# A Strassen-Winograd graph network: M2 accumulated onto M1's copy in PSUM, M5 kept where C22 is built, and W1 read into the room of another tile

## The chip, the cores and the metric

The kernel runs on one core of one Trainium2 chip. The time is device time in microseconds: 2273.53 us, the median of three runs (2271.55 to 2274.96). The profile shows one execution with a span of 2271.4 us. The core has a matrix engine (TensorE, PE in the profile), a vector engine (DVE), a scalar engine (ACT), GpSimd (POOL) and SyncE (SP), which issues most transfers here. They run side by side, each through its own queue in order, and wait for each other on semaphores.

## The reference

Two layers of a graph network, 32 graphs of 512 nodes with 512 features, all in float32:

```
h = relu(layernorm(x));  deg = rowsum(adj)
x = x + relu(concat(h, (adj @ h) / max(deg, 1e-6)) @ W.T)
h = relu(layernorm(x));  q, k = split(h @ Wqk);  v = h @ Wv
w = mask * rowsum(q * (adj @ (k * mask))) / sqrt(512)
x = x + softmax(w over nodes) * v
```

## The kernel before

**Rearranged algebra.** W falls into W1 (for h) and W2 (for the aggregate). Layer 0 first computes `y` = h W2, then `out` = h W1 + A y, with A the adjacency divided by its degrees; relu and the residual follow. In layer 1, q · (adj k) is taken as a row sum of t and u, with `u` = A times the masked h1, and t = h1 (Wq Wk^T); v = h1 Wv. The product of Wq and Wk is made once, so t and v come from one product, `tv`, whose right side holds both matrices side by side (tile `mv`).

**Seven products in place of eight.** Each 512 x 512 product is cut into 2 x 2 blocks and done with seven block products M1 to M7 of Winograd's form of Strassen's algorithm; in `tv` the inner blocks are cut the same way again. Sums of blocks of the left and of the right side (`left_sums`, `right_sums`, L102 to L113, four DVE operations each) are stored in seven slots. The four result blocks share partial sums: M1 + M2 is C11; M1 + M6 is the start of the other three; M1 + M6 + M7 + M5 is C22; M1 + M6 + M5 + M3 is C12; M1 + M6 + M7 + M4 is C21.

**`product` (L118 to L162)** writes this as a generator: it yields after each group of matmuls, so that other work can be put between. It takes three PSUM tiles of one bank each. `pp` gathers M1, then M6, M7 and M4 on top; `pr` holds M2; `pq` holds M5 and then M3. Between these, ACT copies the state of `pp` to SBUF (C11, C12 and C22 so far) and M5 to a block of its own (`m5`), and DVE adds: C11 = copy + `pr`, C22 = copy + `m5`, C12 = copy + `pq`. C21 is taken from `pp` by ACT. The order is M1, M2, M6, M5, M7, M3, M4. In `y` and `u` a block product is 4 matmuls (8 records, as a float32 matmul shows as two); in `out` it is twice that, one half for each of its two terms. `into` (L420) gives where `y` and `u` put the blocks; `layer0_out` (L435) puts them in `block` tiles of the tag `tmp` (four buffers) and adds relu of them to X. `layer1_tv` (L451) is the same scheme with four banks for each of `pp`, `pr` and `pq`; there M5 also goes to blocks, and C22 is `pp` + M5. `layer1_one` does t and v apart, for the last two batches alone.

**Loop.** For batch i the phases follow each other: `out` of i; `tv` of i-1; `u` of i; `y` of i+1. `run` (L167) steps through a phase's generator, and after step n it issues what a `Plan` holds for n. So the order in every queue is written out by hand. A `finish` of a product is issued when its generator is resumed: after the plan's work of that step. In `u`, ahead of C22's add, the plan has DVE turn h1 (`f.turn`), undo the second Strassen level for the lower rows (`post.recombine`, 7 adds) and form four row sums (`post.dot`, L608). In `y` it has DVE turn the adjacency (`fb.turn`), add the softmax terms and undo the level for v.

**W1** does not fit beside everything else. Its seven slots are kept in device memory, and `Stream` (L400) reads them again for each batch into four buffers: four loads are issued at step 0 of `u`, three at steps 1, 3 and 5 of `out`. `tv` (L675) is one tile of 128 x 2 x 2 x 14 x 128 values: row halves, then t or v, then 14 columns of blocks. The t part is last read by `post.dot` in `u` and is written again in the next `tv`.

PSUM is one pool of eight banks (`ps_m`, L72).

Of the kernel before, what the change touches and what calls it, by code (L numbers as in the profile page):

```python
# [16 lines left out]
P = 128  # L17
# [5 lines left out]
def kernel(  # L23
# [32 lines left out]

    nc = tc.nc
    B, N, F = x.shape  # L60
    C = N // P
# [7 lines left out]
    big = ctx.enter_context(tc.tile_pool(name="big", bufs=1))  # L69
    small = ctx.enter_context(tc.tile_pool(name="small", bufs=2))  # L70
    dram = ctx.enter_context(tc.tile_pool(name="dram", bufs=2, space=bass.MemoryType.DRAM))
    ps_m = ctx.enter_context(tc.tile_pool(name="ps_m", bufs=8, space=bass.MemoryType.PSUM))  # L72


    LEFT = {1: 0, 2: 1, 3: 2, 4: 3, 5: 4, 6: 5, 7: 6}
# [3 lines left out]

    PLACE = {2: 0, 3: 1, 4: 2, 7: 3, 1: 4, 6: 5, 5: 6}  # L80
    AT = {p: j for j, p in PLACE.items()}
    ORDER = [1, 2, 6, 5, 7, 3, 4]

    def slots(tag, bufs, name, pool=None):
        return (pool or big).tile([P, 7, 2, H], F32, tag=tag, bufs=bufs, name=name)

    def block(name):
        return big.tile([P, 2, H], F32, tag="tmp", bufs=4, name=name)

    def mm_tile(name):  # L90
        return ps_m.tile([P, 2, H], F32, tag="m", name=name)

    def add(o, a, b, on=None):
        (on or nc.vector).tensor_tensor(o, a, b, op=ALU.add)  # L94
# [4 lines left out]
    def copy(o, i):  # L99
        nc.scalar.activation(o, i, AF.Copy)  # L100
# [14 lines left out]
    def of(t):  # L115
        return lambda i: t[:, i]

    def product(name, terms, place, finish):  # L118

        def m(k, p, first):
            n = 0
            for lt, rt in terms:
                right = rt(k)
                for rc in range(2):
                    for dk in range(2):
                        nc.tensor.matmul(  # L130
                            p[:, rc, :],
                            lt[:, LEFT[k], dk, ts(rc, P)],
                            right[:, dk, :],
                            start=first and n == 0,
                            stop=True,
                            skip_group_check=True,
                        )
                        n += 1
                yield

        pp = mm_tile(f"pp_{name}")
        yield from m(1, pp, True)
        c11 = place(0, 0)
        copy(c11, pp)
        pr = mm_tile(f"pr_{name}")
        yield from m(2, pr, True)
        finish(0, 0, c11, pr, c11)
        yield from m(6, pp, False)
        c12 = place(0, 1)
        copy(c12, pp)  # L150
        pq = mm_tile(f"pq_{name}")
        yield from m(5, pq, True)
        m5 = block(f"m5_{name}")
        copy(m5, pq)
        yield from m(7, pp, False)
        c22 = place(1, 1)
        copy(c22, pp)
        finish(1, 1, c22, m5, c22)
        yield from m(3, pq, False)
        finish(0, 1, c12, pq, c12)  # L160
        yield from m(4, pp, False)
        finish(1, 0, None, pp, None)  # L162

    def right(t):
        return lambda k: t[:, RIGHT[k]]
# [11 lines left out]
    class Later:  # L177


        def __init__(self, tiles, c):  # L180
            self.tiles, self.c = tiles, c
# [103 lines left out]
    class FrontH:  # L285
# [8 lines left out]
        def load(self, h, t=None):  # L294
            self.n[h] = half_tile(f"n_{self.b}_{h}") if t is None else t
            half_rows(self.n[h], x[self.b], h)
# [103 lines left out]
    class Stream:  # L400


        def __init__(self):
            self.d = dram.tile([7, P, 2, H], F32, tag="dw1", bufs=1, name="dw1")
            self.tiles = []
            self.n = 0

        def load(self):
            k = ORDER[self.n % 7]
            t = big.tile([P, 2, H], F32, tag="w1", bufs=4, name=f"w1_{self.n}")  # L410
            nc.sync.dma_start(out=t, in_=self.d[RIGHT[k]])
            self.tiles.append((k, t))
            self.n += 1

        def take(self, k):
            want, t = self.tiles.pop(0)
            assert want == k
            return t

    def into(t):  # L420


        def finish(r, c, o, p, s):
            if s is None:
                copy(t[:, 2 * r + c, :, :], p)
            else:
                add(o, p, s)

        return (lambda r, c: t[:, 2 * r + c, :, :]), finish

    def layer0_y(b):
        y = Y[b] = slots("yh", 1, f"y_{b}")
        return product(f"y_{b}", [(hT, right(w2R))], *into(y))

    def layer0_out(b, w1):  # L435
        def place(r, c):
# [14 lines left out]
    def layer1_tv(b):  # L451

        t = TV[b] = tv
        left = H1T[b]

        def m(k, banks, first):
            for half in ((2, 1), (3, 0)):
                for n in half:  # L460
                    if first:
                        banks[n] = mm_tile(f"ptv_{b}_{k}_{n}")
                    for i, p in enumerate(range(2 * n, min(2 * n + 2, 7))):
                        j = AT[p]
                        nc.tensor.matmul(  # L465
                            banks[n][:, :, ts(i, P)],
                            left[:, LEFT[k], LEFT_IN[j], :],
                            mvR[:, RIGHT[k], RIGHT[j], :, :],
                            start=first and i == 0,
                            stop=True,  # L470
                            skip_group_check=True,
                        )
                yield half

        def part(o, n):
            first = [0, 4, 8, 10][n] + (2 if n < 2 else 3) * (o % 2)
            return t[:, o // 2, :, first:first + min(2, 7 - 2 * n), :].rearrange("p w b f -> p w (b f)")

        def parts(k, banks, first, use):
            for half in m(k, banks, first):  # L480
                yield
                for n in half:
                    use(n, banks[n][:, :, 0:P * min(2, 7 - 2 * n)])

        def keep(o):
            return lambda n, p: copy(part(o, n), p)

        def plus(o):
            return lambda n, p: add(part(o, n), p, part(o, n))

        pp, pr, pq, m5 = {}, {}, {}, {}

        def keep5(n, p):
            m5[n] = block(f"m5_tv_{b}_{n}")[:, :, 0:P * min(2, 7 - 2 * n)]
            copy(m5[n], p)

        yield from parts(1, pp, True, keep(0))
        yield from parts(2, pr, True, plus(0))
        yield from parts(6, pp, False, keep(1))
        yield from parts(5, pq, True, keep5)  # L500
        yield from parts(7, pp, False, lambda n, p: add(part(3, n), p, m5[n]))
        yield from parts(3, pq, False, plus(1))
        yield from parts(4, pp, False, keep(2))

    def layer1_one(b, which, held=None):
# [40 lines left out]
        def plus(o):  # L546
            return lambda n, p: add(part(o, n), p, part(o, n))

        pp, pr, pq, m5 = {}, {}, {}, {}

        def keep5(n, p):
            m5[n] = like(n, block(f"m5_w_{which}_{b}_{n}").rearrange("p a f -> p (a f)"))
            copy(m5[n], p)

        yield from parts(1, pp, True, keep(0))
        yield from parts(2, pr, True, plus(0))
        yield from parts(6, pp, False, keep(1))
        yield from parts(5, pq, True, keep5)
        yield from parts(7, pp, False, lambda n, p: add(part(3, n), p, m5[n]))
        yield from parts(3, pq, False, plus(1))  # L560
        yield from parts(4, pp, False, keep(2))

# [16 lines left out]
    class Post:  # L579
# [71 lines left out]
        def finish(self, r, c):  # L651

            v = self.blocks[r, c]
            for a in range(2):
                o = self.o[:, 2 * r + a, ts(c, H)]
                nc.vector.scalar_tensor_tensor(
                    o, v[:, a, :], self.sm[:, 2 * r + a:2 * r + a + 1], o, op0=ALU.mult, op1=ALU.add
                )
# [88 lines left out]
    def start():  # L747
# [42 lines left out]
            for k in range(2):  # L790
                turn_right(s2[h], h, k, w2R)
        for c in range(C):
            v = block(f"h_{c}").rearrange("p a f -> p (a f)")
            nc.scalar.activation(
                in_order(v), natural(X[0][:, c, :]), AF.Relu, scale=t[1][:, c:c + 1], bias=t[2][:, c:c + 1]
            )
            turn_chunk(v, c, "h")
# [7 lines left out]
        rows = {}  # L805

        def scale_a(c):
            rows[c] = block(f"a_{c}").rearrange("p a f -> p (a f)")
            nc.scalar.activation(
                in_order(rows[c]), natural(fa.n[c // 2][:, c % 2, :]), AF.Copy, scale=fa.rdeg[:, c:c + 1]  # L810
            )
# [122 lines left out]
    with tc.manual_schedule(engines=engines):  # L934
        weights, mvR = start()
        post = None
        for i in range(B):
# [4 lines left out]
            if i > 0:  # L942

                p = Plan()
                for n in range(3):
                    p.at(2 * n + 1, stream.load)
                right_y = right_sums(of(Y[i]))
                p.at(0, right_y[0])
                p.at(0, right_y[2])
# [45 lines left out]
                p.at(12, f.stats, 0)  # L995
                p.at(12, f.stats, 1)
                p.at(13, variance, f.t, 0, 2)
                run(layer0_out(i, stream.take), 14, p)


                post = Post(i - 1, F1[i - 1])
# [55 lines left out]
            if more:  # L1057
                p.at(0, f.turn, 0)
                p.at(1, f.turn, 1)
                p.at(2, FA[i + 1].to.read, 0)  # L1060
                p.at(3, FA[i + 1].to.read, 1)
                for n in range(4):
                    p.at(0, stream.load)
            if i == 0:
                fh = FH[2]
                for c in range(C):
# [38 lines left out]
            if more:  # L1105
# [3 lines left out]
                p.at(3, fb.turn, 1)  # L1109
                p.at(4, fb.sums, 0)  # L1110
                p.at(4, fb.sums, 2)
                p.at(1, load_x, i + 1)
                if i + 2 < B:
                    p.at(5, FH[i + 2].to.read, 0)
# [92 lines left out]
```

## Time and profile before

| | before |
|---|---|
| time, median of 3 | 2273.53 us |
| TensorE busy | 2259.1 us, 99% |
| weight loads (beside the matmuls) | 1978.7 us, 87% |
| DVE busy | 1923.6 us, 85%, 3803 instructions |
| ACT busy | 1025.6 us, 45%, 1896 instructions |
| POOL busy | 174.8 us, 8% |
| DMA, mean | 204 GB/s |
| ACT copies of `m5` in `y`, `u`, `out` | 32 each, 596 to 597 ns |
| DVE adds of C11 in `y`, `u`, `out` | 32 each, 690, 682, 674 ns |
| DVE adds of C22 in `y`, `u`, `out` | 32 each, 684, 684, 685 ns |
| W1 loads | 217 of 256 KB, 4.3 us from issue to landing (median) |

Rows of the profile in order of time have a start, a duration, the engine, the line, the operation, output and inputs by tile name, and in brackets how long the engine had stood idle and which instruction let it go on. Matmul ends are modelled, and a row of several (x8) runs from the first start to the last end, so the start of the next row is the surer number. A DVE record of 0.68 us is followed by the next after about 0.60. The chain is the work that ended last, traced back from the end. A line such as L94 is a helper (`add`), so one goes by the tile names: `xu` is the tile that holds X and later the result of `u`.

### The profile page before, as it was taken

The numbers are of one execution on the slowest core, as the hardware profiler recorded it, in microseconds if no ns is written. First come the engines' busy times: TensorE is split into PE (matmuls) and PEld (weight loads), VectorE is DVE, ScalarE is ACT, GpSimd is POOL, SyncE is SP. The second block draws the span as 40 slices with busy tenths as digits, with TensorE's granted clock in tenths as the row PEclk, the third lists the DMA queues.
The fourth block names the chain that finished last, engine by engine and source line by source line (L and its number), as shares of the span: only waits on it lengthen the run. The fifth ranks groups of instructions, "written<-read, shape, count | busy, mean of one in ns | idle before, by whom it ended". The sixth has DMA issues, their size and how long they took to land.

```text
span 2271.4 us, 32927 instructions
## 1 busy us (share of the span) xinstructions
PE 2259.1 (99%) x10550; PEld 1978.7 (87%) x10550; DVE 1923.6 (85%) x3803; ACT 1025.6 (45%) x1896; POOL 174.8 (8%) x260
## 2 busy tenths in 40 slices
PE   9999999999999999999999999999999999999998
PEld 7788888888888888888888888888888888888897
DVE  7798888888888888888888888888888888888778
ACT  4454443445434554444454344544444543445323
POOL 0000010000100000100000000000000010000000
PEclk9999999999999999999999999999999999999999
DMA  9978787887878777777878888777888787878543
GB/s 222 233 214 246 204 212 193 205 230 206 210 199 202 213 220 207 208 191 207 227 210 205 199 201 218 218 207 202 196 210 225 209 209 193 205 219 217 154 123 96
DMA packets 409773, 463.68 MB, mean 204 GB/s; under 512 B 37729, under 2 KB 271713, under 8 KB 405377
## 3 DMA queue, kind: packets, MB, share of 16 engines
q1 hardware_dynamic: 400192, 428.56, 69.5%
q0 software_dynamic: 8928, 32.51, 8.7%
q8 instruction: 83, 1.36, 0.3%
q14 instruction: 90, 0.73, 0.1%
q10 hardware_dynamic: 480, 0.52, 0.1%
HBM read 293.93 MB, written 167.51 MB: 203 GB/s over the span
## 4 chain that ended last, share of the span: by engine, by line
PE 93%; DMA 3%; DVE 2%; SPq 1%; ACT 0%; issue 0%; DVEq 0%; POOLq 0%; ACTq 0%
PE ptv L465 28%; PE pp_o L130 18%; PE pp_u L130 9%; PE pq_o L130 9%; PE pp_y L130 9%; PE pq_u L130 5%; PE pr_o L130 5%; PE pq_y L130 5%; PE pr_u L130 2%; PE pr_y L130 2%; PE pw L517 1%; DMA a<-in_adj_dram 1%; SPq L212 0%; DVE tv L94 0%; DMA room<-in_L_gnn_Wqk_dram 0%; DVE mv L97 0%
## 5 line engine op out<-in xcount | busy, mean ns | idle before, releaser
L465 PE MATMUL ptv<-mv,h1T 128*128 128x256 f32 x2940 | 639.7, 379 | 0.1
L465 PEld LDWEIGHTS ptv<-mv,h1T 128*128 128x128 f32 x2940 | 558.5, 190 | 76.4 <-DVE xu L444 0.5
L94 DVE TENSOR_TENSOR tv<-tv 128x256 f32<-128x256 f32 (+1 forms) x658 | 326.4, 508 | 13.4 <-ACT tv L100 1.5
L100 ACT ACTIVATE tv<-ptv 128x512 f32<-128x512 f32 (+1 forms) x360 | 184.9, 541 | 262.9 <-PE ptv L465 262.0
L130 PE MATMUL pp_y<-wide 128*128 128x256 f32 x1024 | 242.1, 379 | 1.5 <-ACT y L100 1.2
L130 PE MATMUL pp_u<-h1m,aT 128*128 128x256 f32 x1024 | 242.0, 379 | 0.0
L130 PE MATMUL pp_o<-y,aT 128*128 128x256 f32 x1024 | 241.9, 379 | 0.0
L130 PE MATMUL pp_o<-w,wide 128*128 128x256 f32 x992 | 234.3, 379 | 0.0
L130 PEld LDWEIGHTS pp_y<-wide 128*128 128x128 f32 x1024 | 194.2, 190 | 28.5 <-ACT y L100 1.6
L130 PEld LDWEIGHTS pp_u<-h1m,aT 128*128 128x128 f32 x1024 | 194.4, 190 | 27.0 <-issue 0.7
L130 PEld LDWEIGHTS pp_o<-y,aT 128*128 128x128 f32 x1024 | 194.5, 190 | 26.4
L130 PEld LDWEIGHTS pp_o<-w,wide 128*128 128x128 f32 x992 | 188.5, 190 | 25.6
L100 ACT ACTIVATE o<-pp_o 128x512 f32<-128x512 f32 x96 | 57.2, 596 | 296.0 <-PE pp_o L130 296.0
L100 ACT ACTIVATE y<-pp_y 128x512 f32<-128x512 f32 x128 | 76.3, 596 | 234.5 <-PE pp_y L130 233.4
L94 DVE TENSOR_TENSOR tv<-ptv,tv 128x512 f32<-128x512 f32 x240 | 139.6, 613 | 43.7 <-PE ptv L465 38.4
L97 DVE TENSOR_TENSOR h1T<-h1T 128x512 f32<-128x512 f32 (+2 forms) x193 | 165.8, 873 | 1.2
L100 ACT ACTIVATE xu<-pp_u 128x512 f32<-128x512 f32 x128 | 76.4, 597 | 195.9 <-PE pp_u L130 195.9
L246 POOL TENSOR_TENSOR rstd<-rstd,mhalf 128x2 f32<-128x2 f32 (+1 forms) x96 | 78.7, 820 | 651.0 <-DVE rstd L245 651.0
L130 PE MATMUL pq_y<-wide 128*128 128x256 f32 x512 | 121.0, 379 | 0.0
L130 PE MATMUL pq_o<-y,aT 128*128 128x256 f32 x512 | 121.0, 379 | 0.0
L130 PE MATMUL pq_u<-h1m,aT 128*128 128x256 f32 x512 | 121.0, 379 | 0.0
L94 DVE TENSOR_TENSOR tv<-ptv,m_tv 128x512 f32<-128x512 f32 (+1 forms) x120 | 72.0, 622 | 55.6 <-PE ptv L465 55.1
(130 smaller groups left out, 3269.4 us busy)
## 6 DMA issues: line engine op xcount, KB each, us to landing
w<-dw SPq DMA_DIRECT2D x217, 256.0 KB, 4.3
xu<-in_x_dram SPq DMA_DIRECT2D x128, 256.0 KB, 5.3
a<-in_adj_dram SPq DMA_DIRECT2D x256, 128.0 KB, 3.0
dh1T<-h1m SPq DMA_DIRECT2D x128, 256.0 KB, 3.1
dx<-xu SPq DMA_DIRECT2D x32, 1024.0 KB, 5.1
sh1T<-dh1T SPq DMA_DIRECT2D x256, 128.0 KB, 3.3
shT<-dhT SPq DMA_DIRECT2D x248, 128.0 KB, 6.0
daT<-a SPq DMA_DIRECT2D x124, 256.0 KB, 3.0
```

The source lines that it names most:

```text
L94: (on or nc.vector).tensor_tensor(o, a, b, op=ALU.add)
L97: (on or nc.vector).tensor_tensor(o, a, b, op=ALU.subtract)
L100: nc.scalar.activation(o, i, AF.Copy)
L130: nc.tensor.matmul(p[:, rc, :], lt[:, LEFT[k], dk, ts(rc, P)], right[:, dk, :], start=first and n == 0, stop=True, skip_group_check=True,)
L246: nc.gpsimd.tensor_tensor(rstd[:, a:b], rstd[:, a:b], mhalf[:, a:b], op=ALU.pow)
L465: nc.tensor.matmul(banks[n][:, :, ts(i, P)], left[:, LEFT[k], LEFT_IN[j], :], mvR[:, RIGHT[k], RIGHT[j], :, :], start=first and i == 0, st ...
L517: nc.tensor.matmul(banks[n][:, ts(i, P)], held[:, s, :] if held is not None and j == 3 else left[:, s, LEFT_IN[j], :], mvR[:, RIGHT[k], RI ...
```

## The change

Three things are done together. M2 is accumulated onto a copy of M1 that ACT puts straight into a PSUM bank (`pr`), so that this bank holds C11 when M2 is done; that needs one bank of its own (`ps_r`), with seven left in the other pool. In the first `y` M2 starts its bank afresh as before. M5 comes second instead of fourth and is copied by ACT to the place of C22; after M7 DVE adds `pp` to it, so the separate block and one copy go. And W1's slots are read, all seven, during `y` into the t part of `tv`, which is idle then; the four buffers go. The two spare `tmp` blocks go too, and at the start the turned rows use `tv` as well. The aim is fewer operations on ACT and DVE, less SBUF, and loads of W1 that wait for no buffer.

```diff
-    ps_m = ctx.enter_context(tc.tile_pool(name="ps_m", bufs=8, space=bass.MemoryType.PSUM))
+    ps_m = ctx.enter_context(tc.tile_pool(name="ps_m", bufs=7, space=bass.MemoryType.PSUM))
+    ps_r = ctx.enter_context(tc.tile_pool(name="ps_r", bufs=1, space=bass.MemoryType.PSUM))
...
-    ORDER = [1, 2, 6, 5, 7, 3, 4]
+    ORDER = [1, 5, 6, 2, 7, 3, 4]
...
         pp = mm_tile(f"pp_{name}")
         yield from m(1, pp, True)
-        c11 = place(0, 0)
+        pr = seed_tile(f"pr_{name}")
+        c11 = pr if seed else place(0, 0)
         copy(c11, pp)
-        pr = mm_tile(f"pr_{name}")
-        yield from m(2, pr, True)
-        finish(0, 0, c11, pr, c11)
+        pq = mm_tile(f"pq_{name}")
+        yield from m(5, pq, True)
+        c22 = place(1, 1)
+        copy(c22, pq)
         yield from m(6, pp, False)
         c12 = place(0, 1)
         copy(c12, pp)
-        pq = mm_tile(f"pq_{name}")
-        yield from m(5, pq, True)
-        m5 = block(f"m5_{name}")
-        copy(m5, pq)
+        yield from m(2, pr, not seed)
+        if seed:
+            finish(0, 0, None, pr, None)
+        else:
+            finish(0, 0, c11, pr, c11)
         yield from m(7, pp, False)
-        c22 = place(1, 1)
-        copy(c22, pp)
-        finish(1, 1, c22, m5, c22)
+        finish(1, 1, c22, pp, c22)
         yield from m(3, pq, False)
         finish(0, 1, c12, pq, c12)
         yield from m(4, pp, False)
...
+        def slot(self, k):
+            n = 2 * ORDER.index(k)
+            return tv[:, :, 0, n:n + 2, :].rearrange("p r i f -> p r (i f)")
+
+        def load(self, n):
+            nc.sync.dma_start(out=self.slot(ORDER[n]), in_=self.d[RIGHT[ORDER[n]]])
...
-                        banks[n] = mm_tile(f"ptv_{b}_{k}_{n}")
+                        banks[n] = (seed_tile if n == 0 and k != 1 else mm_tile)(f"ptv_{b}_{k}_{n}")
...
-        yield from parts(5, pq, True, keep5)
-        yield from parts(7, pp, False, lambda n, p: add(part(3, n), p, m5[n]))
+        yield from parts(5, pq, True, keep(3))
+        yield from parts(7, pp, False, plus(3))
...
-                for n in range(3):
-                    p.at(2 * n + 1, stream.load)
...
-                for n in range(4):
-                    p.at(0, stream.load)
...
+                for n in range(7):
+                    p.at(n, stream.load, n)
```

More of the change, by code (lines that the diff above doesn't have):

```diff
@@ L87, in block, with seed_tile @@
     def block(name):
-        return big.tile([P, 2, H], F32, tag="tmp", bufs=4, name=name)
+        return big.tile([P, 2, H], F32, tag="tmp", bufs=2, name=name)
     def mm_tile(name):
         return ps_m.tile([P, 2, H], F32, tag="m", name=name)
+    def seed_tile(name):
+        return ps_r.tile([P, 2, H], F32, tag="r", name=name)
     def add(o, a, b, on=None):
@@ L116, in of, with product @@
         return lambda i: t[:, i]
-    def product(name, terms, place, finish):
+    def product(name, terms, place, finish, seed=True):
         def m(k, p, first):
@@ L404, in __init__ @@
             self.d = dram.tile([7, P, 2, H], F32, tag="dw1", bufs=1, name="dw1")
[L405 to L418, printed above, removed]
+        def slot(self, k):
[3 more added lines that the diff above has]
+            nc.sync.dma_start(out=self.slot(ORDER[n]), in_=self.d[RIGHT[ORDER[n]]])
     def into(t):
@@ L432, in layer0_y @@
         y = Y[b] = slots("yh", 1, f"y_{b}")
-        return product(f"y_{b}", [(hT, right(w2R))], *into(y))
+        return product(f"y_{b}", [(hT, right(w2R))], *into(y), seed=b > 0)
     def layer0_out(b, w1):
@@ L489, in plus @@
             return lambda n, p: add(part(o, n), p, part(o, n))
[L491 to L495, printed above, removed]
+        pp, pr, pq = {}, {}, {}
         yield from parts(1, pp, True, keep(0))
@@ L547, in plus @@
             return lambda n, p: add(part(o, n), p, part(o, n))
[L549 to L553, printed above, removed]
+        pp, pr, pq = {}, {}, {}
         yield from parts(1, pp, True, keep(0))
@@ L557, in layer1_one @@
         yield from parts(6, pp, False, keep(1))
-        yield from parts(5, pq, True, keep5)
-        yield from parts(7, pp, False, lambda n, p: add(part(3, n), p, m5[n]))
+        yield from parts(5, pq, True, keep(3))
+        yield from parts(7, pp, False, plus(3))
         yield from parts(3, pq, False, plus(1))
@@ L792, in start @@
         for c in range(C):
-            v = block(f"h_{c}").rearrange("p a f -> p (a f)")
+            v = tv[:, c // 2, 0, 4 * (c % 2):4 * (c % 2) + 4, :].rearrange("p i f -> p (i f)")
             nc.scalar.activation(
@@ L807, in scale_a @@
         def scale_a(c):
-            rows[c] = block(f"a_{c}").rearrange("p a f -> p (a f)")
+            rows[c] = tv[:, c // 2, 1, 4 * (c % 2):4 * (c % 2) + 4, :].rearrange("p i f -> p (i f)")
             nc.scalar.activation(
@@ L997 @@
                 p.at(13, variance, f.t, 0, 2)
-                run(layer0_out(i, stream.take), 14, p)
+                run(layer0_out(i, stream.slot), 14, p)
                 post = Post(i - 1, F1[i - 1])
```

## The prediction

> **What bounds the kernel now.** I read the page first, then the waits, then the passage from batch 13 to batch 14 in order of time.
>
> ```profile
> PE 2259.1 (99%) x10550; PEld 1978.7 (87%) x10550; DVE 1923.6 (85%) x3803; ACT 1025.6 (45%) x1896; POOL 174.8 (8%) x260
> ...
> PE 93%; DMA 3%; DVE 2%; SPq 1%; ACT 0%; issue 0%; DVEq 0%; POOLq 0%; ACTq 0%
> ```
>
> TensorE is the path. In the chain each batch's `out` product begins 69.50 us after the last one (999.17, then 1068.67), and 322 matmul records (56 in `y`, 112 in `out`, 98 in `tv`, 56 in `u`) at 0.2158 us make 69.5: between batches 3 and 29 TensorE never stops. So nothing taken off DVE or ACT can be won there. Taken away, it can only give room; a new wait of TensorE costs its full length in every batch.
>
> Where DVE waits is the second view (total, times, longest):
>
> ```profile
> DVE tv L94 <- PE ptv L465: 93.5, 137, 2.9
> DVE y L94 <- PE pr_y L130: 87.0, 30, 3.3
> ```
>
> DVE catches up with TensorE twice a batch, at the adds of `tv` and at C11 of `y`. Between those it is late. Here is DVE alone, from the last `tv` add of M3 to C22 of `u`, then TensorE alone:
>
> ```profile
> 972.02 0.69 DVE L94 TENSOR_TENSOR tv<-ptv,tv 128x512 f32<-128x512 f32 x1
> 972.62 2.01 DVE L97 TENSOR_TENSOR h1m<-h1m 128x512 f32<-128x512 f32 x3
> 974.55 0.16 DVE L332 TENSOR_SCALAR deg<-deg 128x2 f32<-128x2 f32 x1
> 974.75 0.17 DVE L333 RECIPROCAL rdeg<-deg 128x2 f32<-128x2 f32 x1
> 974.83 2.91 DVE L94 TENSOR_TENSOR tv<-tv 128x256 f32<-128x256 f32 x7
> 977.66 2.48 DVE L283 STREAM_TRANSPOSE h1T<-sh1T 128x512 f32<-128x512 f32 x4
> 980.07 1.76 DVE L94 TENSOR_TENSOR tv<-tv 128x256 f32<-128x256 f32 x4
> 981.75 0.68 DVE L94 TENSOR_TENSOR xu<-pr_u,xu 128x512 f32<-128x512 f32 x1
> 982.35 1.21 DVE L94 TENSOR_TENSOR tv<-tv 128x256 f32<-128x256 f32 x3
> ...
> 985.92 0.68 DVE L94 TENSOR_TENSOR xu<-m_u,xu 128x512 f32<-128x512 f32 x1
> ```
> ```profile
> 983.47 1.89 PE L130 MATMUL pq_u<-h1m,aT 128*128 128x256 f32 x8
> 985.20 1.89 PE L130 MATMUL pp_u<-h1m,aT 128*128 128x256 f32 x8
> ```
>
> No bracket stands behind any of these DVE rows: the queue is full and waits for nobody. 983.47 is M3 of `u`, 985.20 is M4. The C22 add (`xu<-m_u`) ends at 986.61, **1.41 us after M4 has begun**, and so it is, within 0.1 us, in batches 3 to 29. Today that is harmless, because the add reads the copy of M5 and the copy of C22 in SBUF and M4 waits only for ACT.
>
> [...] one matmul of the last batch's `pw` waits 0.8 us for a DVE add that reads its bank. [...] The longest in this trace after the first product is 1.3 us (two records 1.55 us apart at 89.86), and the records after it keep the 0.216 us step.
>
> **The change, part by part.**
>
> *M2 onto the copy of M1.* In `u` and `y` a DVE add (682 and 690 ns) becomes one more ACT copy (596); in `out` the add goes. The seed copy runs after M1 and M2 is now fourth, two products later (2 x 1.73 us in `u`), and ACT is 45% busy: no wait. Worth 0 on the path, but DVE's queue is 0.60 us shorter ahead of C22 in `u` (981.75 to 982.35), and in `y` the 3.0 us wait for M2 goes.
>
> *M5 in C22's place.* One ACT copy fewer a product. But C22's add now reads `pp`, the bank into which M4 adds, so **M4 waits for DVE instead of ACT**. Behind M4 on TensorE stands everything. Product by product:
>
> `u`: the add ends at 986.61 - 0.60 = 986.01. TensorE came on 0.05 us after the DVE row's end in two waits (`pw` at 2225.89, `ptv` at 124.78), and the next step after such a wait was 0.32 instead of 0.216, so 0.10 more. M4 starts at 986.06 instead of 985.20 and loses **0.96 us**. DVE is pinned anew by the `tv` adds of the next batch (972.02 is the end of M3), so this comes back each time.
>
> `y`: before, the add ran at 997.88 and M4 at 997.28, late as well. After, M4 stands at 998.24 (0.96 later). DVE runs the first transpose at 987.1 instead of 991.26; the sum of exponents then waits for ACT's exponent, which follows the seed copy after M1 (989.6 + 0.6 + 0.3 = 990.5). From there: transpose 1.2, two recombinations 1.3, two sums 1.3, the weights 0.4, two recombinations 1.3: 996.1. M7 ends at 996.5, the add at 997.2. 1.0 us to spare: no wait.
>
> `out`: the add ends 1.6 us before M4 in batches 3 to 29. No wait. `tv` already adds from `pp` after M7, so there only the copy's address changes.
>
> *Order M1 M5 M6 M2 M7 M3 M4.* `out` needs the right sum s1 - s0 of Y two products earlier. DVE has it by 1001.7; M5's second half starts at 999.0 + 5.2 = 1004.2. No wait.
>
> *Seven PSUM banks and one.* `product` holds two in the pool of seven, `tv` four plus three, as it frees them now. No wait.
>
> *W1 in `tv`.* Seven loads of 256 KB move into `y`. DMA is full there (share 1.02 from 982 to 998) and nearly empty at 999 to 1002 (0.11). A load has 128 packets of 2 KB, about 113 ns each in the packet records of this batch; in two pieces of 1 KB (47.7 ns each) some 0.8 us of all 16 engines a load, 5 to 6 us for seven. The rest is pushed to about 1004. The first is needed at 1000, twelve us after its issue; the others 3.45 us apart, behind 1.73 us of issue. The transposes' data are issued ahead of them. 0, with 0 to 1 us a batch as bounds. Two tiles interleaved in one buffer could wait for each other falsely; the mask rows do not (ACT writes two interleaved blocks of `h1m` back to back at 1026.90, before the first is even sent at 1030.66), so I take none.
>
> *The start and the end.* Read in the same way. `y` of batch 0: M5 needs a left sum that DVE ends at 18.86, +0.4, and M4 waits for an add that ended 1.43 late, +1.1: 1.5. `u` of 0: the add ended 6.19 late behind two transposes that wait for DMA; less the C11 add, and with up to 1.1 for W1's loads gone from the DMA queue, 4.7 to 5.6: 5.2 [...]. This gives back waits of 1.4 (M7 of `y` 1, the gap at 89.86) and 0.4 (`ptv` at 124.78). `u` of 1: 0.85. `y` of 2: late 5.33 behind DMA that now goes out 1.9 earlier, and 0.85 by the shift: 2.5. Sum 8.7, between 4 and 12. Batch 30: 0.7. Batch 31 and the tail: M4 of `u` 1.4 later, DVE's closing chain two adds shorter: 0.3.
>
> **Sum.** Batches 2 to 29: 28 x 0.96 = 26.9. With 8.7 + 0.7 + 0.3: 36.6. 2273.5 + 36.6 = **2310 us**, 1.6% slower.
>
> **Rivals.** *DVE's lateness is absorbed* (ended on the other side): the shorter queue and idle DMA let DVE reach C22 before M3 ends; against it, 13.3 us of work without one wait from 972.6 to 985.9, of which 0.6 goes. Only the waits of 1.4 and 0.4 and half a us of tail would move: 2271. *The wait in `u` only, the start swallows its part:* 2273.5 + 26.9 = 2300. *`y` stalls as well*, because the exponent or W1's loads hold DVE or TensorE: 30 batches by about 0.5 more: 2325. *False waits between W1 and the value half of `tv`*: a DMA round trip (4.3 us) or more a batch: 2400 and up.
>
> **Chances.** Forecast 0.74, start swallowed 0.10, `y` as well 0.08, false waits 0.02, absorbed 0.06. The range takes in the start's 4 to 12, 0.85 to 1.05 us a batch, and the second case: 2296 to 2320. Slower by over 0.2% (4.5 us) 0.92, same 0.04, faster 0.04.
>
> **What would show it.** Right: a wait of M4 (`pp_u`) for the DVE add of `xu` of about 0.85 us (0.96 with the slow second step), some 30 times; batch period 70.4 us; no wait of `y` for `pr_y`; `pp_y` and `pp_o` without waits after batch 2. Wrong: a period of 69.5 (absorbed), DVE ahead of M4 in `u`; waits of `pp_o` for W1's DMA or of DVE for it; a wait of `pp_y`. The forecast fails if DVE starts the stretch before C22 earlier than the last `tv` add lets it.

## The result and the profile after

The changed kernel takes **2307.57 us** (median of four, 2306.18 to 2309.41) against 2273.93 (the three runs above and one more, 2271.55 to 2274.96): ratio **1.015**, 95% interval 1.0132 to 1.0168. The forecast was 2310, the range 2296 to 2320. A run's time is 1.8 us above the span of its profile, here 2307.6 us.

First the page: busy times, then the shares of the chain.

```profile
PE 2270.2 (98%) x10550; PEld 1978.2 (86%) x10550; DVE 1880.0 (81%) x3707; ACT 1006.7 (44%) x1862; POOL 175.1 (8%) x260
...
PE 77%; DVE 19%; issue 2%; DMA 1%; SPq 0%; ACT 0%; DVEq 0%; POOLq 0%; POOL 0%; ACTq 0%
```

The work that was to go is gone: DVE does 96 instructions less and is busy 43.6 us less, ACT 34 less and 18.9 us. The share of busy time says nothing more than that. The chain says what happened: DVE's part of it rises from 2% to 19%. The chain now crosses to DVE in every batch. A share of the chain is not a loss: these 19% are some 13.7 us a batch, the DVE stretch shown below, and only the part of it in which TensorE stands still is lost.

The waits name the crossing (total, times, longest; PEld is the weight load ahead of the same matmul):

```profile
DVE tv L100 <- PE ptv L466: 94.0, 128, 2.9
PEld pp_u L136 <- DVE xu L100: 37.6, 32, 3.5
PE pp_u L136 <- DVE xu L100: 24.7, 32, 3.1
...
PE pp_y L136 <- DVE y L100: 1.3, 1, 1.3
```

Thirty-two waits of `pp_u`, one in each batch, for DVE's add into `xu`. DVE's wait in `y` for `pr_y` (87.0 us before) is no longer there. Now the same passage as before, DVE from the middle of the masking of h1 to C22 of `u`, then TensorE:

```profile
990.23 2.01 DVE L103 TENSOR_TENSOR h1m<-h1m 128x512 f32<-128x512 f32 x3
992.16 0.16 DVE L339 TENSOR_SCALAR deg<-deg 128x2 f32<-128x2 f32 x1
992.36 0.17 DVE L340 RECIPROCAL rdeg<-deg 128x2 f32<-128x2 f32 x1
992.44 2.92 DVE L100 TENSOR_TENSOR tv<-tv 128x256 f32<-128x256 f32 x7
995.27 2.48 DVE L290 STREAM_TRANSPOSE h1T<-sh1T 128x512 f32<-128x512 f32 x4
997.68 2.89 DVE L100 TENSOR_TENSOR tv<-tv 128x256 f32<-128x256 f32 x7
...
1002.93 0.69 DVE L100 TENSOR_TENSOR xu<-pp_u,xu 128x512 f32<-128x512 f32 x1
```
```profile
1001.08 1.89 PE L136 MATMUL pq_u<-h1m,aT 128*128 128x256 f32 x8
1003.67 1.99 PE L136 MATMUL pp_u<-h1m,aT 128*128 128x256 f32 x8 [0.70 <-DVE xu L100]
1005.50 1.89 PE L136 MATMUL pp_y<-wide 128*128 128x256 f32 x8
```

The C11 add has gone from between the recombinations of `tv`, and the stretch from 990.23 to the end of the C22 add (1003.62) is 13.39 us long; before it was 13.99. Still no bracket stands behind any DVE row: the queue is full. M3 starts at 1001.08, so M4 was due at 1002.81. It starts at 1003.67, which is 0.05 after DVE's row ends: 0.86 lost, and 0.10 more at the second record. That is 0.968 us of 70.47, the time from this M4 to that of the next batch (1074.14).

In the steps between TensorE's records one can add up what it loses, as step less 0.216 us. Before, 3.7 us in the whole run; after, 41.6. The 37.9 between them, less 1.75 us that DVE's closing chain became shorter, are the 36.2 us between the two profiled spans. Nothing is left over.

### The profile page after: what moved, and what is told of

It reads as the page before. It is cut to its first block, busy times and chain, and to the rows that moved or that the text cites. A ratio compares the mean times of both kernels' runs of the same rounds, so it can differ in the third digit from the quotient of the medians.

```text
span 2307.6 us, 33009 instructions
## 1 busy us (share of the span) xinstructions
PE 2270.2 (98%) x10550; PEld 1978.2 (86%) x10550; DVE 1880.0 (81%) x3707; ACT 1006.7 (44%) x1862; POOL 175.1 (8%) x260
## 2 busy tenths in 40 slices
DMA packets 437550, 463.70 MB, mean 201 GB/s; under 512 B 37728, under 2 KB 327264, under 8 KB 433152
## 4 chain that ended last, share of the span: by engine, by line
PE 77%; DVE 19%; issue 2%; DMA 1%; SPq 0%; ACT 0%; DVEq 0%; POOLq 0%; POOL 0%; ACTq 0%
PE ptv L466 24%; PE pp_o L136 19%; PE pq_o L136 10%; PE pp_y L136 9%; DVE tv L100 8%; PE pr_o L136 5%; PE pq_y L136 5%; DVE h1T L290 3%; DVE tv L604 3%; PE pp_u L136 3%; DVE h1m L103 2%; PE pr_y L136 2%; PE pw L514 1%; DVE xu L100 1%; DMA room<-in_L_gnn_W_dram 0%
## 5 line engine op out<-in xcount | busy, mean ns | idle before, releaser
L106 ACT ACTIVATE tv<-ptv 128x512 f32<-128x512 f32 x480 | 241.3, 546 | 379.1 <-PE ptv L466 379.1
L100 DVE TENSOR_TENSOR tv<-ptv,tv 128x512 f32<-128x512 f32 (+1 forms) x360 | 212.1, 616 | 103.0 <-PE ptv L466 94.0
L136 PE MATMUL pp_u<-h1m,aT 128*128 128x256 f32 x1024 | 247.0, 384 | 24.7 <-DVE xu L100 24.7
L136 PE MATMUL pp_o<-tv,wide 128*128 128x256 f32 x992 | 234.3, 379 | 0.0
L136 PEld LDWEIGHTS pp_o<-tv,wide 128*128 128x128 f32 x992 | 188.5, 190 | 25.6
L263 ACT ACTIVATE n<-n,nmr,rstd 128x512 f32<-128x512 f32 x120 | 88.2, 802 | 117.2 <-DMA out_dram<-tv 84.1
L106 ACT ACTIVATE xu<-pp_u 128x512 f32<-128x512 f32 x64 | 38.2, 598 | 194.4 <-PE pp_u L136 194.4
L136 PE MATMUL pq_o<-tv,wide 128*128 128x256 f32 x496 | 117.2, 379 | 0.0
L106 ACT ACTIVATE y<-pp_y 128x512 f32<-128x512 f32 x65 | 38.9, 598 | 174.3 <-PE pp_y L136 174.3
```

Of the source, the lines that this page charges most:

```text
L136: nc.tensor.matmul(p[:, rc, :], lt[:, LEFT[k], dk, ts(rc, P)], right[:, dk, :], start=first and n == 0, stop=True, skip_group_check=True,)
L263: nc.scalar.activation(o, i, AF.Relu, scale=t[1][:, c:c + 1], bias=t[2][:, c:c + 1])
```

## The experiments

The theory: all that is lost is M4's wait for DVE at C22's add in `u`, with stops of the same kind in batch 0 and in the last batch; what makes it is M5 in C22's place alone, and how large it is depends on what DVE has to do ahead of that add. Rivals: part of the loss comes from W1's transfers, from the PSUM banks or from the new order of the products.

**M5 in its own block, all else as changed.** The changed kernel with one edit in `product` (and four `tmp` buffers again; `tv` stays as changed):

```diff
-        c22 = place(1, 1)
-        copy(c22, pq)
+        m5 = block(f"m5_{name}")
+        copy(m5, pq)
...
-        finish(1, 1, c22, pp, c22)
+        c22 = place(1, 1)
+        copy(c22, pp)
+        finish(1, 1, c22, m5, c22)
```

> The changed kernel with one part undone: M5 goes to a block of its own again, ACT copies C22 out of pp after M7, and DVE adds the two in SBUF (four tmp blocks again). The seed in PSUM, the order M1 M5 M6 M2 M7 M3 M4 and W1 in tv stay. Theory (M4 waits for the DVE add that reads pp): the 0.97 us in u of every batch goes, batch period 69.5 us, no wait of pp_u for xu, the 6.5 us in u of batch 0 go too; 2271 us, between 2268 and 2275. Rival (the seed, the order or W1's loads are the cause): the period stays near 70.4 and the time near 2305.

Measured: 2273.81 us against 2273.02, ratio 1.0007 (0.9998 to 1.0016). In the list of waits none of `pp_u` or `pp_y` for DVE is left. Here are DVE and TensorE in the same place:

```profile
986.04 0.69 DVE L100 TENSOR_TENSOR xu<-m_u,xu 128x512 f32<-128x512 f32 x1
```
```profile
984.19 1.89 PE L136 MATMUL pq_u<-h1m,aT 128*128 128x256 f32 x8
985.91 1.89 PE L136 MATMUL pp_u<-h1m,aT 128*128 128x256 f32 x8
987.64 1.89 PE L136 MATMUL pp_y<-wide 128*128 128x256 f32 x8
```

DVE is as late as in the changed kernel: its add ends at 986.73, 0.82 after M4 has begun. But it reads two SBUF tiles, and M4 starts 1.72 us after M3, without a stop. The edit restores one ACT copy a product (ACT is busy 1060.5 us instead of 1006.7), which nobody waits for. So the seed of M2, the new order, the banks 7 + 1 and W1 together cost at most 0.16% by that interval, and nothing that the profile shows in a regular batch (the period is 69.50 us).

**The opposite: M5 in C22's place alone.** The kernel before, in `product` only:

```diff
-        m5 = block(f"m5_{name}")
-        copy(m5, pq)
+        c22 = place(1, 1)
+        copy(c22, pq)
         yield from m(7, pp, False)
-        c22 = place(1, 1)
-        copy(c22, pp)
-        finish(1, 1, c22, m5, c22)
+        finish(1, 1, c22, pp, c22)
```

> The kernel before with this one part of the change in product: M5 is copied to the place of C22 and DVE adds pp to it after M7. Order, M2 in a bank of its own with the add of C11, and W1's four buffers as before. Theory: M4 now meets DVE where it stood before, 1.41 us late in u and 1.28 in y, and each wait costs 0.15 more: 1.56 + 1.43 = 3.0 us a batch, period 72.5, with some 8 us of the start: about 2365 us (2350 to 2380), far slower than the whole change. Rival (the seed brings nothing, as it is off the path): about the same as the whole change, 2308.

Measured: **2376.58 us**, ratio 1.0456 (1.0441 to 1.0472), inside the range and 12 us over the middle of it.

```profile
DVE y L94 <- PE pr_y L130: 140.8, 31, 4.6
DVE tv L94 <- PE ptv L463: 97.8, 141, 2.9
PEld pp_u L130 <- DVE xu L94: 57.2, 32, 4.6
PEld pp_y L130 <- DVE y L94: 51.7, 31, 4.3
```

Two products wait now. In `u` TensorE loses 1.57 us in a regular batch: 0.97 and the 0.60 of the C11 add, which stands ahead of C22 on DVE again. In `y` it loses 1.44: there the C11 add holds DVE until M2 is done, and what follows it comes too late for M4. This is the 3.0 us a batch that I expected (the period is 72.50), so the 12 us lie outside the regular batches, at the start above all. DVE in `y`:

```profile
1042.88 0.69 DVE L94 TENSOR_TENSOR y<-pr_y,y 128x512 f32<-128x512 f32 x1 [4.57 <-PE pr_y L130]
1043.49 1.23 DVE L276 STREAM_TRANSPOSE aT<-saT 128x1024 f32<-128x1024 f32 x1
```

DVE stands idle for 4.57 us with the transposes queued behind the waiting add. The whole change, with the seed, the new order and W1's move beside M5 in C22's place, is 69 us faster than this run (2376.58 - 2307.57), although these three showed no gain in the first experiment. Of the 69 us, 57 are 28 regular batches of 2.04 us (0.60 in `u`, 1.44 in `y`), and in both places the trace shows the C11 add on DVE that the seed takes away. That the seed does it without the new order was not run. DVE's wait for M2 matters only once TensorE waits for DVE: an edit's price depends on the other edits.

**Row sums behind the add.** If DVE's place in its queue is the cause, the loss must shrink by what is taken from ahead of the add. In the changed kernel the four row sums of `u` (0.61 us each) are issued at steps 3, 3, 4, 4; the add comes after the work of step 4.

```diff
-                    p.at(3 + c // 2, post.dot, c)
+                    p.at([3, 3, 4, 5][c], post.dot, c)
```

> The changed kernel, but one of the four row sums of u (post.dot, 0.61 us of DVE each) is issued after the add of C22 instead of ahead of it, in batches 1 to 30. Nothing is left out. Theory (M4's wait is the DVE work queued ahead of the add): the wait falls by 0.61, from 0.97 to about 0.36 us a batch, period 69.86; 30 x 0.61 = 18 us less: 2289 us (2286 to 2292). Rival (a fixed cost of the wait or of reading pp): under 5 us less, 2303 or more.

Measured: 2289.95 us, ratio 1.0073 (1.0058 to 1.0088); a regular batch loses 0.355 us, against 0.968: 0.613 less, one row sum.

With two of them behind the add (`[3, 3, 5, 5][c]`):

> As the run with one row sum later, but with two of the four after the add of C22. Theory: the add ends 0.3 us before M4, the wait is gone in batches 1 to 30, period 69.5; 2279 us (2276 to 2282), what is left over the kernel before being the start, mainly u of batch 0. Rival (a fixed cost, or the row sums then hold up something else, such as W1's loads or the scores): 2290 or more.

Measured: 2281.05 us, ratio 1.0032 (1.0021 to 1.0042). The profile has not one wait of `pp_u` in batches 1 to 30:

```profile
987.54 0.69 DVE L100 TENSOR_TENSOR xu<-pp_u,xu 128x512 f32<-128x512 f32 x1
```
```profile
986.91 1.89 PE L136 MATMUL pq_u<-h1m,aT 128*128 128x256 f32 x8
988.64 1.89 PE L136 MATMUL pp_u<-h1m,aT 128*128 128x256 f32 x8
```

The add ends at 988.23, 0.41 before M4 is due. The profiled span is 2276.3; what it has over the kernel before is mainly the stop of 3.8 us in `u` of batch 0. The median is 2 us over the middle of the expectation. The granted clock goes with it: six of the eight executions ran at a mean of 0.998 and took 2280.6 to 2281.8 us, the two at 0.999 and 1.000 took 2275.9 and 2278.2. Only the one at 1.000 was profiled, so a stretch at half the clock in the six is likely but not shown. The last section comes back to this.

**W1 alone.** The kernel before with the seven loads of `y` into `tv`, nothing else:

```diff
-                for n in range(3):
-                    p.at(2 * n + 1, stream.load)
...
-                for n in range(4):
-                    p.at(0, stream.load)
...
+                for n in range(7):
+                    p.at(n, stream.load, n)
```

> The kernel before with one part of the change alone: W1's seven slots read in `y` into the t part of `tv`; the seven products keep their order, m5 its block and M2 its DVE add. Theory (W1's move is hidden by TensorE): no wait of `pp_o`, `pr_o` or `pq_o` for DMA, batch period 69.50, 2273 us, within 1.5 of before, although DMA stays full some 20 us longer in each batch. Rival (the loads hold up the transposes of `y` or the products of `out`): 0.3 us or more in each of 30 batches, 2282 us and up. SyncE's waits for TensorE ahead of the loads go in both.

Measured: 2275.47 us against 2273.64, ratio 1.0009 (1.0001 to 1.0017): 1.8 us more, just outside the 1.5 that I had allowed. Batches 2 to 29 lose nothing, as expected. Batch 1 does, which neither the theory nor the rival had. ACT, then TensorE, in `out` of batch 1:

```profile
108.66 0.63 ACT L328 ACTIVATE a<-a 128x512 f32<-128x512 f32 x1 [2.03 <-DMA a<-in_adj_dram]
109.20 0.19 ACT L328 ACTIVATION_READ_ACCUMULATOR a<-a 128x1 f32 x1
109.29 0.61 ACT L328 ACTIVATE a<-a 128x512 f32<-128x512 f32 x1
109.81 0.19 ACT L328 ACTIVATION_READ_ACCUMULATOR a<-a 128x1 f32 x1
109.90 0.57 ACT L100 ACTIVATE o<-pp_o 128x512 f32<-128x512 f32 x1
```
```profile
106.39 1.89 PE L130 MATMUL pq_o<-y,aT 128*128 128x256 f32 x8
110.53 3.68 PE L130 MATMUL pp_o<-tv,wide 128*128 128x256 f32 x8 [2.25 <-ACT o L100]
```

No matmul waits for W1. All seven loads of W1 now go out ahead of the last parts of an adjacency's load; its last part is issued 2.8 us later and lands 4.1 us later than before (108.56 instead of 104.48). ACT waits for that (the row began at 104.66 before, at 108.66 here), and the copy of C12 out of `pp_o`, for which M7 has to wait, stands behind it in ACT's queue. In the first experiment the same wait is 1.9 us. In the changed kernel it does not show; TensorE comes to this place later there, which I take for the reason.

**The stop of batch 0.** In the changed kernel four pairs of statistics of batch 2 stand ahead of the add in `u` of batch 0:

```diff
-                    p.at(2 + c, fh.stats, c)
-                p.at(5, variance, fh.t)
+                    p.at(5 + c // 2, fh.stats, c)
+                p.at(6, variance, fh.t)
                 p.at(6, shift, fh.t)
-                p.at(6, weights[0])
```

(with `weights[0]` put ahead of them, at step 5).

> The changed kernel, with four pairs of DVE statistics (3.4 us) in `u` of batch 0 put behind C22's add instead of ahead of it, and the sums of W2 that follow ahead of them. Nothing else moves; batches 1 to 31 are as they are. Theory (the stop of 3.2 us was one of DVE's queue, and the 14 records at half the rate after it were the price of the stop's length): the wait of M4 falls to under 1.2 us, all records after it keep the 0.216 us step, and the time falls by 2.5 of wait and 3.3 of clock, to 2302 us (2300.5 to 2304). Rival 1 (the two transposes of h1 wait for DMA so long that M4 waits anyway): 2307. Rival 2 (the half rate comes from something else than the stop): the wait falls and the half rate stays, 2305.

Measured: 2304.85 us, ratio to before 1.0138 (1.0124 to 1.0152): 2.7 us less than the changed kernel, where I expected 5.8 from 2.5 of wait and 3.3 of clock (the trace has 3.0 for the clock). It is outside the range, and by its number at the second rival's 2305; but that rival kept the half rate, and in the trace the half rate is gone. What failed is the wait, which falls only to 2.1 us:

```profile
81.57 1.31 DVE L290 STREAM_TRANSPOSE h1T<-sh1T 128x512 f32<-128x512 f32 x2 [3.74 <-DMA sh1T<-dh1T]
82.80 0.65 DVE L100 TENSOR_TENSOR xu<-pp_u,xu 128x512 f32<-128x512 f32 x1
```

The first rival has a part in it: DVE reaches the add straight from the transposes, and they wait for DMA. In the changed kernel their data came at 80.42, here at 81.57; why 1.15 later I did not find out. Also, three of the changed kernel's four executions had a granted clock of 0.999 rather than the 0.998 of the profiled one, so its median probably holds less of the half rate than its profile does.

**Together.** Two row sums and the statistics later, and three small moves in the first and last batch:

> The changed kernel with two row sums later in each `u`, the statistics later in `u` of batch 0, and three edits to the first and the last batch (the order of the first sums on DVE, the sums of the right side of Y in `y` of batch 0 one step later, the inner sums of the last `u` one step later). If what was lost is DVE's lateness at C22's add and nothing else, TensorE's waits fall from 41.6 us to about 4 to 6, the DVE chain at the end is two adds shorter than before, and the time is 2270 to 2273 us: even with the kernel before or 0.1% under it. Rival (the freed room of ACT and DVE is worth something of its own): under 2268. Rival (a new wait comes up behind the removed ones): 2277 and up.

Measured: 2275.8 us against 2273.64, ratio 1.001 (1.0002 to 1.0018). TensorE loses 6.7 us instead of 41.6. (The small move in `y` of batch 0 is of W1's sums, by two steps, not of Y's by one, as the expectation has it.) It does not beat the kernel before: the time lies between the theory's 2273 and the 2277 of new waits. What is left is 2.0 us of M4 in `u` of batch 0 (the transposes again) and 0.7 earlier in that product, 0.8 in `out` of batch 1, which is the ACT wait of W1 alone, now uncovered, 0.5 in `y` of batch 2, 1.9 in the last batch's `v`, and 0.8 of `pw` that before has too. The freed ACT and DVE time showed no worth of its own.

## Why the prediction was right, step by step

**`u`, the main term: right in mechanism and size.** Predicted 0.96 us a batch, from 1.41 of lateness, less 0.60 for the C11 add, plus 0.05 and 0.10. Measured 0.968 (0.864 + 0.104), 27.1 us for batches 2 to 29 against 26.9. The premise was that DVE is pinned by the `tv` adds and does not catch up; the row sums show it from one side (0.61 us less ahead of the add, 0.61 less wait) and the second experiment from the other (0.60 more, 0.60 more). One reading was wrong without harm: after the wait of `pw` at 2225.89 the second step is 0.214 us, not 0.32; as the other steps there are 0.111, it is still 0.10 more.

**`y` and `out`: right, in `y` more narrowly than I thought.** No wait after batch 0. The C22 add of `y` ends 0.76 us before M4 (predicted 1.0), and with the C11 add on DVE, in the old order, there is a wait in every batch, as the second experiment shows. In `out` it ends 2.5 us before M4 (1.6 before).

**Order, banks, ACT's copies: right, nothing.** ACT's copy into PSUM takes 582 ns; I had reckoned with the 596 of the copy to SBUF, an estimate, as no row of before has a copy into PSUM.

**W1 in `tv`: right for the changed kernel.** The loads take 7.3 us to land instead of 4.3, the number of packets rises from 409773 to 437550, and DMA is full from 1000 to 1024 (shares of 1.10, 1.18 and 1.19). The old end at 998 is near 1016 here, so the full stretch runs some 8 us on, longer than the 5 to 6 us of extra work that I had put behind it. It stays hidden, but for batch 1 as soon as nothing else delays TensorE. No false wait reached TensorE, and SyncE's waits for TensorE ahead of the loads fall from 334 us in all (225 of them for `pp_o`) to 17.

**The start: the sum about right, its terms not.** Predicted 8.7, measured 6.8 in the profiled execution:

| | predicted | measured |
|---|---|---|
| `y` of 0, less 0.55 that before lost there | 1.5 | 1.95 |
| `u` of 0, less 0.36 before | 5.2 + 0.5 for the clock | 3.0 + 3.0 for the clock |
| given back | -1.8 | -1.8 |
| `u` of 1 | 0.85 | 0.70 |
| `y` of 2 | 2.5 | 0 |

Two terms failed for the same step left out: a loss moves TensorE, and the next wait shrinks by as much. In `u` of 0 the add ends at 84.81 instead of 86.07, as early as I thought, but M4 was due at 81.62 instead of 79.88, because of what `y` of 0 had lost; so the wait is 3.2 us and not 5.2. The clock drop I had put too low: the 0.5 us for it in the sum of 8.7 was my estimate, which nothing in the trace of before showed; it cost 3.0. In `y` of 2 I moved TensorE by 0.85 us only, the loss in `u` of 1, and not by what it had lost in batch 0. In the changed kernel its M4 comes at 170.27 instead of 163.31, 6.96 later, while the second transpose, which waits for DMA in both, starts 1.32 later (163.83 instead of 162.51); the add ends at 169.95, in time. An early loss is lost once, and gives the DMA room further on: in the combined kernel, which loses less in batch 0, `y` of 2 waits 0.5 us.

**The end: mis-sized.** Predicted 0.7 + 0.3. Measured: 0.70 in batch 30, 1.42 in `u` of batch 31, 1.8 more in front of M4 of `v`, and 1.75 given back after the last matmul: 0.7 + 1.5. The wait in `v` costs nothing by itself, as DVE's chain ends the run either way.

The sum in the profiled execution is 36.2 us (predicted 36.6); in the medians it is 33.6. Three of the four executions were 1.0 to 3.2 us under the profiled one, which fits a stretch at half rate that comes in some of them only.

## What to carry to other kernels

When an edit lets an engine read an accumulating bank instead of a copy, look at when that read ends today against the next matmul into the bank: lateness that was free becomes a wait of the bottleneck engine in every round (0.97 us of 70.47 here), however many instructions the edit removes (96 of DVE's here). Cost it from the queue: the end of the last row that is pinned, plus what stands ahead of the read; and moving work behind the read bought it back one for one here (0.613 us for a row sum of 0.61), until nothing was left to wait for. Price edits in the company in which they come: the seed, the order and W1's move gained nothing beside a copy of M5, and 69 us beside M5 in C22's place.

## What the runs showed of the hardware

**The half rate after a stop.** In `u` of batch 0 TensorE stood 3.2 us over its step, and after a step of 0.59 us the next thirteen took 0.427 us instead of 0.216. The windows of the changed kernel after that stop show the granted clock in the column ahead of the DMA share:

```profile
84.80:88.00 3.20, 3.14 (x7) 2.53 (x8) 2.50 (x7) 0.00 (x0) 1.18 (x2) 0.50 0.89 231
88.00:91.20 3.20, 3.20 (x9) 2.57 (x8) 2.83 (x4) 0.60 (x1) 0.00 (x0) 0.53 1.02 278
91.20:95.00 3.80, 3.80 (x19) 3.34 (x18) 2.40 (x3) 1.88 (x3) 0.00 (x0) 1.00 0.28 65
```

Over all profiles, stops of 2.1, 2.4, 3.2, 3.9, 4.0 and 4.4 us had such a stretch after them (six to thirteen full steps of 0.427 us); another of 2.1 us, one of 1.9 and one of 3.7 us, with two row sums later, had none:

```profile
84.51 1.99 PE L136 MATMUL pp_u<-h1m,aT 128*128 128x256 f32 x8 [3.52 <-DVE xu L100]
86.34 1.89 PE L136 MATMUL pp_y<-wide 128*128 128x256 f32 x8
```

So the length of a stop does not decide it: W1 alone had the drop after 2.4 us, where two row sums later had none after 3.7. Here are the windows, first W1 alone, where TensorE comes on again at 110.53, then two row sums later, where it does at 84.51:

```profile
110.50:112.00 1.50, 1.47 (x4) 1.20 (x5) 1.50 (x1) 0.46 (x1) 0.00 (x0) 0.55 0.00 0
112.00:114.00 2.00, 2.00 (x6) 1.57 (x5) 1.97 (x5) 1.33 (x2) 0.00 (x0) 0.50 0.00 0
114.00:116.00 2.00, 2.00 (x11) 1.75 (x10) 1.97 (x4) 0.03 (x1) 0.00 (x0) 0.98 0.70 262
```
```profile
84.80:88.00 3.20, 3.20 (x16) 2.81 (x16) 2.51 (x7) 0.60 (x1) 1.18 (x2) 1.00 0.86 242
88.00:91.20 3.20, 3.20 (x17) 2.81 (x16) 3.13 (x4) 1.79 (x3) 0.00 (x0) 1.00 1.05 248
```

The first number behind the comma is TensorE's busy time: 11 records in 2.00 us once the clock is back, 6 in 2.00 us before. The six and two executions of two row sums later, at mean clocks of 0.998 against 0.999 and 1.000, suggest that the same stop can have the drop in one execution and not in another. What decides it was not shown: this is read from nine traces, and no run was made to vary it.

**Restart.** After nearly every wait the second step is 0.29 to 0.32 us, 0.07 to 0.10 more than the others, if the clock stays full; in the waits of M4 it is 0.32.

**Smaller packets.** W1's 1 KB packets took 64.5 ns each on average and 2 KB ones 138 ns in the same stretch (1000 to 1024; over the whole batch, with others, 58.7 and 116): half the size took about half the time. So it is likely that the loads took longer to land because they share a full stretch with the transposes, and not because of a price per packet.
